# Attention phase of a Mamba and attention chain: second layer with keys on the partitions and a constant shift, head steps in pairs, own slots for the outer stages

## The chip, the core and the metric

The kernel runs on one core of one Trainium2 chip. Its engines are TensorE (PE in the profile, with PEld for its weight loads), VectorE (DVE), ScalarE (ACT), GpSimd (POOL) and SyncE (SP), which issues the DMAs. The metric is the device time of one execution in microseconds (us), the median of several.

## The reference, cut to what matters

Eight images of 256 channels and 32x32 pixels (1024 tokens) pass through four layers; all is float32.

```python
# layer 0: four Mamba blocks, a squeeze-and-excite gate, batch norm    (not touched)
# layer 1: four heads of 64 dimensions
attn = softmax(einsum('bihd,bjhd->bijh', q, k) * 64 ** -0.5, axis=2)
x = (einsum('bijh,bjhd->bihd', attn, v) @ w_out + b_out) + x
# layer 2: one head of 256 dimensions, on the negated energies
energy = einsum('bnc,bmc->bnm', x @ Wq.T + bq, x @ Wk.T + bk)
attention = softmax(max(energy, axis=-1) - energy, axis=-1)
x = gamma * einsum('bnm,bmc->bnc', attention, x @ Wv.T + bv) + x
# layer 3: position encoding, eight heads of 32 dimensions, output projection
x = x + pe;  out = softmax(q k / sqrt(32)) v;  y = out @ Wo.T + bo
```

A softmax doesn't change if one constant is subtracted from all the exponents of a row, so any shift that keeps the exponentials inside float32 gives the same result.

## The kernel before

`mamba_phase` computes layer 0 and spills each image to HBM. `attention_phase` then does layers 1 to 3 for all images in one interleaved stream. A recording layer (`Engines`, `InOrder`) keeps every engine's instructions in the order in which the program states them, and gives them all the line L48 in the profile; so the reader goes by tile names. SP alone is not held to that order.

**Stages.** `order` lists 16 calls of `heads`: layer 1 of image 0, layer 1 of image 1, layer 3 of image 0, layer 1 of image 2, layer 3 of image 1, and so on; the last two are layer 3 of images 6 and 7. Each call is called a stage here. Beside its heads a stage carries pieces of two generators: `ends(i)`, what follows the stage before it, and `begins(i)`, what the next stage needs. Beside the heads of layer 3 stand `residual` and the whole of `layer2` of the next image, and the loading, normalization and `qkv` projections of layer 1 of the image after it. Beside the heads of layer 1 stand `output` of the last layer 3 and `qkv` of the next.

**Heads.** 128 channels hold 2 heads of layer 1 or 4 of layer 3; `pairs` is 1 or 2. A step is one block of 128 keys (`kt`) for 512 queries (`half`) of one channel group (`m`), 32 steps in a stage. `weights` (part `"fs"`) multiplies keys by queries on 64 or 32 rows of the array for each head, the heads at the same time, into tiles `fs` of two PSUM banks (pool `ps_s`, 2 buffers), and ACT writes the exponentials `fp`. `product` (`"fo"`), one step later, multiplies values by `fp` on 64 or 32 columns of the array into the accumulator `fo` (pool `ps_o`, 4 buffers, shared with all projections), and sums `fp` over the key blocks into `fz`, on DVE for the first pair of heads and on POOL for the second. After 8 steps `divide` (`"z"`) sums `fz` over the partitions by a matmul with `ones` into `fzs`, takes the reciprocal `frec` on DVE, multiplies `fo` by it into the tile `fq`, and has POOL compare `frec` with two bounds into `ok`.

**Slots.** Between its parts, `heads` yields slot numbers, three for each step: `3 * i + 0, 1, 2`. In the middle stages `BESIDE_H` says at which slots the next piece of `end` or `begin` is put in; in the first two and last two stages the pieces of both are spread evenly, `PIECES = 52` for 96 slots. What is left over follows after the last slot. `PARTS_H` gives the order of the parts within a step, for 1 and 2 pairs.

**Layer 2.** `qkv` makes `fq` (the weights of query and key are multiplied beforehand into `wqk`, so x itself is the key) and `fv`. For each block of 128 queries, `energies` multiplies queries by keys into an `fs` tile with the queries on the partitions, and DVE takes the row minimum `fe`; `weights` has ACT compute the exponential with this minimum as its bias and the row sum; `scale` multiplies the row by gamma over the sum; `turn` transposes the row by eight transposes on TensorE (`ft`) and copies it (`fpt`); `product` multiplies by the values, 128 columns at a time, into `fo`, and DVE adds x. At the end POOL adds the position encoding, which makes x ready for layer 3.

At the end of the phase the minimum of `ok` becomes a flag; if a comparison failed anywhere, `general_attention` computes the three layers again in a form that takes a row maximum everywhere.

## Time and profile before

| | us |
|---|---|
| Median of 3 runs | 8681.78 (8677.01 to 8682.0) |
| Profiled execution | 8677.8 |
| Its span (first to last instruction) | 8676.0 |
| First attention matmul | 6272.8 |
| TensorE busy in the span | 8420.9 |
| DVE, POOL, ACT busy | 7188.4, 6924.9, 5504.7 |

The page's rows of 40 slices show each engine's busy share in tenths; a slice is 217 us here, and the attention phase begins at the 29th. A matmul in float32 stands as two instructions in the profile, and heads that run at the same time on parts of the array start 6 or 7 ns apart. The end of a matmul is modelled; the start of the next one is not, so lengths on TensorE are best read from start to start. In a line such as `fs<-fq,fk 64*128 64x512 f32 x4`, 64*128 is the part of the array (rows * columns), 64x512 the moving operand, x4 the number of instructions in a row.

### The profile page before, as it was taken

How to read it: one execution, taken by the hardware profiler on the slowest of the kernel's cores; microseconds unless marked ns; L12 is line 12 of the kernel's file. 1: busy time of each engine (PE TensorE's matmuls, PEld its weight loads, DVE VectorE, ACT ScalarE, POOL GpSimd, SP SyncE). 2: the span in 40 equal slices, each digit the busy share in tenths (PEclk: the TensorE clock that was granted, in tenths of full speed). 3: DMA queues.
4: the chain of work that ended last, by engine and by line, in shares of the span. 5: the costliest groups of instructions: out<-in, count | busy, mean ns of one | idle time of the engine just before them, and what ended most of it. 6: DMA issues, size and time to landing. Idle time of an engine off the chain costs nothing. (4 is left out here: it accounts for less than half of the span.)

```text
span 8676.0 us, 230366 instructions
## 1 busy us (share of the span) xinstructions
PE 8420.9 (97%) x100338; PEld 4366.5 (50%) x100338; DVE 7188.4 (83%) x7175; ACT 5504.7 (63%) x7805; POOL 6924.9 (80%) x2513
## 2 busy tenths in 40 slices
PE   8999999999999999999999999999799999999998
PEld 4555555555555555555555555555444344434432
DVE  5999999999999999999999999999755655565555
ACT  6777777777777777777777777777433334433434
POOL 5999999999999999999999999999713434343436
PEclk9999999999999999999999999999899999999999
DMA  3444444444444444444444444444400000000000
GB/s 116 130 130 128 127 133 134 130 129 128 131 127 129 134 131 130 127 132 126 128 134 133 127 144 140 138 135 138 145 1 6 10 6 8 8 6 6 3 3 11
DMA packets 558037, 841.33 MB, mean 97 GB/s; under 512 B 311328, under 2 KB 312416, under 8 KB 556384
## 3 DMA queue, kind: packets, MB, share of 16 engines
q1 hardware_dynamic: 557024, 826.52, 31.4%
q8 instruction: 795, 13.03, 0.6%
q14 instruction: 218, 1.79, 0.1%
HBM read 771.31 MB, written 55.05 MB: 95 GB/s over the span
## 5 line engine op out<-in xcount | busy, mean ns | idle before, releaser
L48 POOL TENSOR_TENSOR h<-h,ct 128x2048 f32<-128x2048 f32 x1022 | 4634.4, 4553 | 168.9 <-DVE hc L48 80.3
L48 ACT ACTIVATE da<-dt,A 128x512 f32<-128x512 f32 x4096 | 2641.7, 713 | 267.7 <-DVE h L48 267.0
L48 PEld LDWEIGHTS bx<-dg,dtxT 64*64 64x64 f32 x65536 | 1889.7, 133 | 1268.4 <-issue 1126.9
L48 DVE TENSOR_TENSOR_SCAN h<-da,hc,bx 128x512 f32<-128x512 f32 x2048 | 2454.8, 1261 | 61.3 <-PE bx L48 31.2
L48 DVE TENSOR_TENSOR_SCAN h<-da,bx 128x512 f32<-128x512 f32 x2048 | 2354.8, 1203 | 95.5 <-PE bx L48 77.0
L48 PE MATMUL bx<-dg,dtxT 64*64 64x128 f32 x65536 | 2221.8, 272 | 64.4 <-DVE h L48 34.7
L48 PE MATMUL y<-h,twin 64*64 64x512 f32 x16384 | 1956.4, 590 | 8.1 <-DVE h L48 4.7
L48 ACT ACTIVATE fp<-fs 128x1024 f32<-128x1024 f32 x768 | 759.5, 1021 | 1168.4 <-PE fs L48 1136.2
L48 PE MATMUL pin<-xn,win 128*128 128x512 f32 x2048 | 1005.7, 614 | 59.4 <-ACT sz L48 48.2
L48 PEld LDWEIGHTS y<-h,twin 64*64 64x64 f32 x16384 | 614.5, 133 | 631.3 <-issue 616.8
L48 POOL TENSOR_TENSOR fz<-fz,fp 128x1024 f32<-128x1024 f32 x192 | 485.1, 2526 | 434.2 <-ACT fp L48 430.2
L48 PE MATMUL fs<-fq,fk 32*128 32x512 f32 (+1 forms) x3072 | 636.7, 655 | 29.5 <-ACT fp L48 27.8
L48 DVE TENSOR_TENSOR fz<-fz,fp 128x1024 f32<-128x1024 f32 x384 | 597.8, 1557 | 77.8 <-ACT fp L48 69.1
L48 DVE SCALAR_TENSOR_TENSOR xin<-pin,vec,xin 128x509 f32<-128x509 f32 (+2 forms) x768 | 572.4, 745 | 61.3 <-ACT xin L48 21.9
L48 PE MATMUL fo<-fp,fv 128*32 128x512 f32 (+1 forms) x3072 | 563.6, 621 | 3.2 <-ACT fp L48 1.6
L48 PEld LDWEIGHTS pin<-xn,win 128*128 128x128 f32 x2048 | 349.9, 190 | 424.7 <-issue 282.8
L48 PE MATMUL po<-sz,wo 128*128 128x512 f32 x1024 | 486.5, 608 | 0.8 <-DVE sz L48 0.8
L48 ACT ACTIVATE sz<-pin,ib 128x512 f32<-128x512 f32 x256 | 175.8, 687 | 418.9 <-PE pin L48 418.9
L48 ACT ACTIVATE xin<-pin,cb,vec 128x512 f32<-128x512 f32 x256 | 199.0, 777 | 288.5 <-PE pin L48 288.5
L48 PEld LDWEIGHTS fs<-fq,fk 32*128 32x128 f32 (+1 forms) x3072 | 178.3, 187 | 391.8 <-issue 236.9
L48 POOL TENSOR_TENSOR e<-e,one 128x1024 f32<-128x1024 f32 x128 | 304.1, 2376 | 87.5 <-ACT one L48 84.1
L48 ACT ACTIVATE e<-pd,vec 128x512 f32<-128x512 f32 x256 | 176.1, 688 | 292.9 <-PE pd L48 290.8
(395 smaller groups left out, 8279.3 us busy)
## 6 DMA issues: line engine op xcount, KB each, us to landing
ct<-cdr SPq DMA_DIRECT2D x1024, 512.0 KB
dg<-diagonals SPq DMA_DIRECT2D x512, 256.0 KB
spill<-xo SPq DMA_DIRECT2D x64, 512.0 KB
x<-spill SPq DMA_DIRECT2D x48, 512.0 KB
xo<-spill SPq DMA_DIRECT2D x48, 512.0 KB
x<-in_x SPq DMA_DIRECT2D x16, 512.0 KB
res<-in_x SPq DMA_DIRECT2D x16, 512.0 KB
diagonals<-bt SPq DMA_DIRECT2D x512, 4.0 KB
```

What stands on the lines that cost most here:

```text
L48: return self.tc.keep_in_program_order(getattr(self.engine, name)(*args, **kwargs))
```

## The change

- **Layer 2** puts keys on the partitions. `weights` makes energies of two key blocks for 512 queries, and ACT writes exponentials `fp` with the constant `shift` of -40; row minimum, row sums, `scale` and `turn` are gone. `product` accumulates the output over the key blocks in two `ps_o` tiles of 512 columns, while POOL sums the exponentials; `divide`, once for each half of the queries, sums over the partitions with `ones` (now 128 columns wide), divides on DVE, and POOL adds x. Gamma is multiplied into the value weights and bias at the start of the phase, on ACT.
- **Heads** go through two steps per iteration, with six slots. In layer 1 the two `weights` stand together, ahead of the products; in layer 3 they stay apart. `divide` follows in the same iteration as the product that completes the sum.
- **The range test** keeps the least and the most of the sums themselves (`least`, `most`), on DVE, in place of POOL's four operations; the bounds are tested at the end.
- **Slots**: new lists for the middle stages, and lists of their own for the first two and the last two stages. The pool `fp` has 10 buffers in place of 8.

```diff
-PARTS_H = {1: ("fs", "z", "fo", "0", "1", "2"), 2: ("0", "fs", "fo", "z", "1", "2")}
+PARTS_H = {
+    1: ("fs0", "fs1", "fo0", "z", "0", "1", "2", "3", "4", "5", "fo1"),
+    2: ("0", "fs0", "fo0", "z", "1", "2", "3", "fs1", "fo1", "4", "5"),
+}
+
 
 BESIDE_H = {
-    3: (("end", (3, 5, 6, 8, 10, 14, 15, 15, 16, 22, 27, 28, 28, 28, 28, 29, 30, 42, 42, 42, 44, 48, 48, 50, 52, 54, 59, 59, 60, 62, 65, 66, 68, 69, 69, 75, 76, 76, 80, 83)),
-        ("begin", (40, 44, 50, 52, 55, 55, 63, 70, 78, 83, 86, 88, 91))),
-    1: (("end", (16, 16, 38, 41)),
-        ("begin", (37, 39, 43, 44, 52, 56, 64, 74, 79, 83, 87, 89))),
+    3: (
+        ("end", (2, 4, 7, 9, 12, 14, 17, 20, 23, 24, 24, 30, 34, 34, 36, 41, 44, 44, 46, 49, 51, 55, 55, 58, 60, 63, 65, 65, 71, 73, 79)),
+        ("begin", (24, 31, 39, 43, 54, 55, 66, 67, 70, 77, 86, 90, 92)),
+    ),
+    1: (
+        ("end", (10, 10, 26, 42)),
+        ("begin", (36, 43, 46, 46, 54, 57, 68, 75, 85, 85, 87, 88)),
+    ),
+    "first": (
+        ("begin", (10, 16, 22, 28, 34, 40, 46, 53, 59, 65, 71, 77, 83)),
+    ),
+    "second": (
+        ("end", (2, 2, 14, 20, 26, 26, 28, 29, 33, 36, 36, 36, 38, 39, 39, 39, 39, 45, 50, 50, 50, 51, 52, 54, 56, 56, 56, 61, 62, 63, 63, 63, 63, 64, 64, 65, 67, 71, 72)),
+        ("begin", (72, 72, 76, 76, 78, 88, 89, 89, 91, 93, 95, 97)),
+    ),
+    "late": (
+        ("end", (1, 2, 4, 7, 10, 10, 12, 14, 16, 19, 19, 22, 26, 29, 30, 30, 35, 36, 39, 40, 42, 43, 45, 45, 48, 48, 48, 50, 56, 58, 58, 60, 61, 61, 61, 61, 66, 66, 67)),
+        ("begin", (72, 77, 79, 86, 89, 89, 89, 91, 93, 97, 98, 102)),
+    ),
+    "last": (
+        ("end", (20, 22, 22, 46)),
+    ),
 }
-
-PIECES = 52
...
-    pp = ctx.enter_context(tc.tile_pool(name="f_p", bufs=8))
+    pp = ctx.enter_context(tc.tile_pool(name="f_p", bufs=10))
-    l2 = ctx.enter_context(tc.tile_pool(name="f_l2", bufs=2))
...
-    ones = cst.tile([P, 64], F32, name="ones")
+    ones = cst.tile([P, P], F32, name="ones")
     nc.gpsimd.memset(ones, 1.0)
-    ok = cst.tile([P, T], F32, name="ok")
-    nc.gpsimd.memset(ok, 1.0)
+    least = cst.tile([P, T], F32, name="least")
+    nc.gpsimd.memset(least, 1.0)
+    most = cst.tile([P, T], F32, name="most")
+    nc.gpsimd.memset(most, 1.0)
+
+    shift = cst.tile([P, 1], F32, name="shift")
+    nc.gpsimd.memset(shift, -40.0)
...
+    def extremes(z):
+
+        nc.vector.tensor_tensor(least, z, least, ALU.min)
+        nc.vector.tensor_tensor(most, z, most, ALU.max)
...
-        probs, acc = {}, {}
+        probs, acc, summed = {}, {}, []
...
-        def divide(i):
-            m, half, kt = steps[i]
-            if kt < TT - 1:
-                return
-            del probs[i]
+            if kt == TT - 1:
+                del probs[i]
+                summed.append((m, half))
+
+        def divide(m, half):
             z = ps_o.tile([P, T], F32, name=f"fzs{u}_{m}_{half}", tag="o")
             for h in range(2 * pairs):
                 r = h * D
...
             nc.vector.reciprocal(rec, z)
 
             nc.vector.tensor_tensor(q[:, m, half * T:(half + 1) * T], acc.pop((m, half)), rec, ALU.mult)
-            for op, bound in ((ALU.is_le, 1e25), (ALU.is_ge, 1e-37)):
-                f = sp.tile([P, T], F32, name=f"fok{u}_{m}_{half}_{bound}", tag="f")
-                nc.gpsimd.tensor_scalar(f, rec, bound, None, op)
-                nc.gpsimd.tensor_tensor(ok, ok, f, ALU.mult)
+            extremes(z)
 
         lag = LAG[pairs]
-        for i in range(len(steps) + lag + 1):
+        for i in range(0, len(steps) + lag + 2, 2):
             for part in PARTS_H[pairs]:
-                if part == "fs":
-                    if i < len(steps):
-                        weights(i)
+                if part[:2] == "fs":
+                    if i + int(part[2]) < len(steps):
+                        weights(i + int(part[2]))
+                elif part[:2] == "fo":
+                    if lag <= i + int(part[2]) < len(steps) + lag:
+                        product(i + int(part[2]) - lag)
                 elif part == "z":
-                    if 0 <= i - lag - 1:
-                        divide(i - lag - 1)
-                elif part == "fo":
-                    if lag <= i < len(steps) + lag:
-                        product(i - lag)
+                    for g in summed:
+                        divide(*g)
+                    summed.clear()
                 else:
                     yield 3 * i + int(part)
 
...
     def layer2(b, x):
+
         s = {}
         yield from qkv(2, b, x, bias2, None, s)
         q, v = s["q"], s["v"]
-        ps, ws, es, pts = {}, {}, {}, {}
-
-        def energies(t):
-            sc = ws[t] = ps_s.tile([P, 2, T], F32, name=f"fs2{b}_{t}", tag="s")
-            for half in range(2):
+        steps = [(half, a) for half in range(2) for a in range(TT // 2)]
+        probs, acc = {}, {}
+
+        def weights(half, a):
+            sc = ps_s.tile([P, 2, T], F32, name=f"fs2{b}_{half}_{a}", tag="s")
+            for j in range(2):
+                t = 2 * a + j
                 for m in range(CT):
-                    nc.tensor.matmul(sc[:, half, :], lhsT=q[:, m, t * P:(t + 1) * P], rhs=x[:, m, half * T:(half + 1) * T],
+                    nc.tensor.matmul(sc[:, j, :], lhsT=x[:, m, t * P:(t + 1) * P], rhs=q[:, m, half * T:(half + 1) * T],
                                      start=(m == 0), stop=(m == CT - 1))
-            e = es[t] = l2.tile([P, 1], F32, name=f"fe2{b}_{t}", tag="e")
-            nc.vector.tensor_reduce(e, sc, AX.XY, ALU.min)
-
-        def weights(t):
-            p = ps[t] = l2.tile([P, HW], F32, name=f"fp2{b}_{t}", tag="p2")
-            z = es[t, "z"] = l2.tile([P, 1], F32, name=f"fz2{b}_{t}", tag="z")
-            nc.scalar.activation(p, ws.pop(t).rearrange("p h t -> p (h t)"), AF.Exp, bias=es.pop(t), scale=-1.0, accum_out=z)
-
-        def scale(t):
-
-            z = es.pop((t, "z"))
-            nc.vector.reciprocal(z, z)
-            rz = l2.tile([P, 1], F32, name=f"frz2{b}_{t}", tag="rz")
-            nc.scalar.activation(rz, z, AF.Identity, scale=gamma)
-            nc.scalar.activation(ps[t], ps[t], AF.Identity, scale=rz)
-
-        def turn(t):
-            p = ps.pop(t)
-            pt = pts[t] = l2.tile([P, TT, P], F32, name=f"fpt2{b}_{t}", tag="pt")
-            for g in range(2):
-                tr = ps_o.tile([P, TT // 2, P], F32, name=f"ft2{b}_{t}_{g}", tag="o")
-                for j in range(TT // 2):
-                    kt = g * TT // 2 + j
-                    nc.tensor.transpose(tr[:, j, :], p[:, kt * P:(kt + 1) * P], ident)
-                nc.vector.tensor_copy(pt[:, g * TT // 2:(g + 1) * TT // 2, :], tr)
-
-        def product(t):
-            pt = pts.pop(t)
-            po = ps_o.tile([P, CT, P], F32, name=f"fo2{b}_{t}", tag="o")
+            p = probs[half, a] = pp.tile([P, 2, T], F32, name=f"fp2{b}_{half}_{a}", tag="p")
+            nc.scalar.activation(p, sc, AF.Exp, bias=shift, scale=-1.0)
+            yield
+
+        def product(half, a):
+            if a == 0:
+                acc["o"] = [ps_o.tile([P, T], F32, name=f"fo2{b}_{half}_{m}", tag="o") for m in range(CT)]
+            p = probs[half, a]
             for m in range(CT):
-                for kt in range(TT):
-                    nc.tensor.matmul(po[:, m, :], lhsT=v[:, kt, m * P:(m + 1) * P], rhs=pt[:, kt, :],
-                                     start=(kt == 0), stop=(kt == TT - 1))
-            nc.vector.tensor_tensor(q[:, :, t * P:(t + 1) * P], po, x[:, :, t * P:(t + 1) * P], ALU.add)
-
-        for i in range(TT + 2):
-            if i < TT:
-                energies(i)
-                yield
-            if 0 <= i - 2:
-                product(i - 2)
-            if i < TT:
-                weights(i)
-            yield
-            if 0 <= i - 1 < TT:
-                turn(i - 1)
-            if i < TT:
-                scale(i)
-            yield
-
-        nc.gpsimd.tensor_tensor(x, s["q"], pe, ALU.add)
+                for j in range(2):
+                    nc.tensor.matmul(acc["o"][m], lhsT=v[:, 2 * a + j, m * P:(m + 1) * P], rhs=p[:, j, :],
+                                     start=(a == 0 and j == 0), stop=(a == TT // 2 - 1 and j == 1))
+                if m == 0:
+                    yield
+            if a == 1:
+                acc["z"] = zp.tile([P, 2, T], F32, name=f"fz2{b}_{half}", tag="z2", bufs=2)
+            if a:
+                nc.gpsimd.tensor_tensor(acc["z"], acc["z"] if a > 1 else probs[half, 0], p, ALU.add)
+                probs.pop((half, a - 1))
+            yield
+
+        def divide(half):
+            z = ps_o.tile([P, T], F32, name=f"fzs2{b}_{half}", tag="o")
+            for j in range(2):
+                nc.tensor.matmul(z, lhsT=ones, rhs=acc["z"][:, j, :], start=(j == 0), stop=(j == 1))
+            rec = sp.tile([P, T], F32, name=f"fr2{b}_{half}", tag="rec")
+            nc.vector.reciprocal(rec, z)
+            sl = slice(half * T, (half + 1) * T)
+            for m in range(CT):
+                nc.vector.tensor_tensor(q[:, m, sl], acc["o"][m], rec, ALU.mult)
+            extremes(z)
+            nc.gpsimd.tensor_tensor(q[:, :, sl], q[:, :, sl], x[:, :, sl], ALU.add)
+            acc.clear()
+            del probs[half, TT // 2 - 1]
+            yield
+
+        for i in range(len(steps) + 1):
+            if i < len(steps):
+                yield from weights(*steps[i])
+            if i:
+                yield from product(*steps[i - 1])
+                if steps[i - 1][1] == TT // 2 - 1:
+                    yield from divide(steps[i - 1][0])
+
+        nc.gpsimd.tensor_tensor(x, q, pe, ALU.add)
         yield
 
...
+    nc.scalar.activation(w["wv2"], w["wv2"], AF.Identity, scale=gamma)
+    nc.scalar.activation(bv[2], bv[2], AF.Identity, scale=gamma)
     w["wq2"] = cst.tile([P, CT, C], F32, name="wqk2")
     bias2 = cst.tile([P, CT], F32, name="bias2")
...
         D = 64 if n == 1 else 32
         ends, nexts = end(i), begins(i)
-        regular = 0 < i and i + 1 < len(order) and order[i - 1][0] == order[i + 1][0] == (3 if n == 1 else 1)
-        both = chain(ends, nexts)
-        count = 0
+        kind = {0: "first", 1: "second", len(order) - 2: "late", len(order) - 1: "last"}.get(i, n)
+        rest = {"end": ends, "begin": nexts}
         for slot in heads(n, b, state[n, b], D, D ** -0.5):
-            if regular:
-                for (what, when), g in zip(BESIDE_H[n], (ends, nexts)):
-                    for _ in range(when.count(slot)):
-                        next(g, None)
-            else:
-                while count * 96 < PIECES * slot:
-                    next(both, None)
-                    count += 1
-        for _ in both:
+            for what, when in BESIDE_H[kind]:
+                for _ in range(when.count(slot)):
+                    next(rest[what], None)
+        for _ in chain(ends, nexts):
             pass
     for _ in output(B - 1, state[3, B - 1]):
         pass
 
 
+    ends = cst.tile([P, 2], F32, name="ends")
+    nc.vector.tensor_reduce(ends[:, 0:1], least, AX.X, ALU.min)
+    nc.vector.tensor_reduce(ends[:, 1:2], most, AX.X, ALU.max)
+    nc.vector.tensor_scalar(ends[:, 0:1], ends[:, 0:1], 1e-25, None, ALU.is_ge)
+    nc.vector.tensor_scalar(ends[:, 1:2], ends[:, 1:2], 1e37, None, ALU.is_le)
     low = cst.tile([P, 1], F32, name="low")
-    nc.vector.tensor_reduce(low, ok, AX.X, ALU.min)
+    nc.vector.tensor_tensor(low, ends[:, 0:1], ends[:, 1:2], ALU.mult)
     ps = ps_o.tile([P, T], F32, name="fcount", tag="o")
     nc.tensor.matmul(ps[0:1, 0:1], lhsT=low, rhs=ones[:, 0:1], start=True, stop=True)
     nc.vector.tensor_scalar(top, ps[0:1, 0:1], P - 0.5, None, ALU.is_lt)
```

## The prediction

> **What bounds the kernel now.** I read the page first, then the attention phase in windows, one for each stage of heads, then TensorE's timeline inside one stage of each kind.
>
> ```profile
> span 8676.0 us, 230366 instructions
> PE 8420.9 (97%) x100338; PEld 4366.5 (50%) x100338; DVE 7188.4 (83%) x7175; ACT 5504.7 (63%) x7805; POOL 6924.9 (80%) x2513
> PE   8999999999999999999999999999799999999998
> PEclk9999999999999999999999999999899999999999
> ```
>
> The change touches only what comes after the first attention matmul, at 6272.8 us; the rest of the span, 2403 us, is what it can move. There TensorE is at 9 tenths in every slice but the last. A busy TensorE can still hide lost time, so the windows come next.
>
> ```profile
> core 0: us, PE busy (x) PEld busy (x) DVE busy (x) ACT busy (x) POOL busy (x), PEclk, DMA share, GB/s
> 6299.06:6582.65 283.59, 276.97 (x1122) 116.88 (x1121) 150.46 (x148) 90.00 (x100) 50.29 (x29) 0.98 0.00 1
> 7351.93:7451.93 100.00, 99.44 (x354) 31.37 (x353) 65.56 (x52) 32.64 (x32) 31.19 (x17) 1.00 0.06 21
> 7451.93:7641.75 189.82, 186.58 (x1058) 88.49 (x1056) 104.86 (x100) 87.50 (x100) 91.30 (x44) 0.99 0.00 1
> 8319.62:8527.55 207.93, 194.71 (x1058) 89.91 (x1056) 103.12 (x100) 82.70 (x96) 97.58 (x45) 0.98 0.00 1
> 8527.55:8659.23 131.68, 108.47 (x565) 28.12 (x561) 75.58 (x40) 62.51 (x64) 106.00 (x44) 0.88 0.02 9
> ```
>
> The rows are: the first two stages (both layer 1); one layer 1 stage; one layer 3 stage (with layer 2 of another image beside it); the last but one; the last. Six middle stages of each kind alternate; layer 1 always takes 100.0, layer 3 188.2 to 191.2 (mean 189.5). In the middle no other engine is near its limit; only in the last stage is POOL (106.0 of 131.7) beside TensorE.
>
> ```profile
> 7062.12 1.99 PE L48 MATMUL fs<-fq,fk 64*128 64x512 f32 x8
> ...
> 7101.95 1.13 PE L48 MATMUL fs<-fq,fk 64*128 64x512 f32 x4
> 7103.01 1.08 PE L48 MATMUL fo<-fp,fv 128*64 128x512 f32 x4
> 7104.02 3.70 PE L48 MATMUL fwk<-fx,wk 128*128 128x512 f32 x8
> 7107.65 1.13 PE L48 MATMUL fs<-fq,fk 64*128 64x512 f32 x4
> ```
>
> Take start to start, not the modelled durations. A full-array `fwk` run of 8 instructions (each matmul is two) takes 3.63: 8 x 0.43 + 0.19. Two concurrent heads of `fs`, two passes: 1.06 = 2 x 0.43 + 0.2. So a pass of 512 columns costs 0.43 and each change of tile shape about 0.185. Where two `fs` steps stand together (7062.12, at a stage's start) no change lies between them. From the same spacing, `fwv` (256 columns) costs 0.216 and a 128-column instruction 0.11.
>
> **Check of the price list.** A middle layer 1 stage has (instructions taken from the built order) 136 passes of concurrent heads, 48 full passes, 32 of 256 columns and 73 shape changes: 184 x 0.43 + 32 x 0.216 + 73 x 0.185 = 99.5; measured 100.0. Layer 3: 136 + 128 passes, 64 of 256, 320 of 128 columns, 90 changes: 113.5 + 13.8 + 35.2 + 16.7 = 179.2 (summed from the finer spacings 178.4); measured 189.5, so 11 us of each are waits. The first two stages: 271.3 against 283.6. Last but one: 179.4 against 207.9. Last, with its tail: 85.8 against 148.4.
>
> **The change, TensorE's work.** Layer 2, per image: 64 transposes and 256 product instructions of 128 columns go (320 x 0.11 = 35.2); 64 product passes of 512 columns and 8 of `ones` come (72 x 0.43 = 31.0): -4.2. The energies only swap roles (64 passes both ways). Shape changes, counted in the built order: layer 1 middle 73 -> 48, as `fs0 fs1` stand together and `fo1` often meets the next iteration's `fs`/`fo`; first 71 -> 56; second 96 -> 62; layer 3 middle 90 -> 93 (its two steps are not merged, and the pieces are smaller); last but one 96 -> 90; last 67 -> 67. With 0.185 each: layer 1 -4.6 x 6; layer 3 -4.2 + 0.5 = -3.7 x 6; first -2.8; second -10.5; last but one -5.3: **-68** in all; the finer spacings give **-65**.
>
> **Waits, layer 3 middle.**
>
> ```profile
> 7503.00 1.13 PE L48 MATMUL fs<-fq,fk 32*128 32x512 f32 x4
> 7505.62 1.13 PE L48 MATMUL fs<-fq,fk 32*128 32x512 f32 x4 [1.50 <-ACT fp L48]
> 7506.68 1.79 PE L48 MATMUL fo<-fp,fv 128*32 128x512 f32 x8
> 7508.40 2.06 PE L48 MATMUL fs<-fq,fk 32*128 32x512 f32 x8
> ```
>
> Layer 2's energies hold one of the two `s` buffers until DVE's minimum and then the exponential are done (in this stage ACT waited 25.2 us in total for `fe`), so the heads' `fs` waits for a buffer. With the constant shift the exponential follows the matmul directly: this stall goes. What is late next: iterations with no piece between two `fs` (slots 25-27, 82-84, 94-96) where two exponentials of 1.02 outlast `fo`'s 0.9-1.0, up to 1 us each; the `ones` product behind POOL's last sum at the stage's end, about 2.4 with the wait of `fo` before it, as now; two places where layer 2's two accumulators, the heads' `fo` and a `fzs` hold all four `o` buffers until DVE has done reciprocal (3.36) and products (0.69 each). I take 7 of the 11 us (bounds 3 and 12): 175.2 + 7 = 182.2, **-44** over six.
>
> **Waits, layer 1 middle.** `z` now follows `fo0` directly. Before it PE has `fo`, `fs fs`, `fo0` = 4.8 us after the last `fs`; exponential and two DVE sums need 1.1 + 2 x 1.56 = 4.2, so it just fits; at the stage's end, where no `fs` is left, about 1 us shows. DVE per stage: 28 sums x 1.56, 4 x (3.36 + 0.69), the new extremes 8 x 0.69, 16 evacuations x 0.72, layer 2's last division 6.1: 83 of 95 us. I take 1.5 (0.5 to 4): 95.9, **-25** over six. DVE's new work hides under TensorE here; if DVE fell behind, each us would show.
>
> **First two.** The begin pieces no longer start at slot 0, where `fwq` waited 3.5 for x, then ran at half rate (8.6 in all). New: in the second stage, layer 2's `final` and the next `qkv` stand in one slot, 72. From the last `fzs2`: reciprocal 3.36, two products 1.38, POOL adds x (128x1024, 2.5) and the encoding (5.47): 12.7 us until x is there, with 4.8 us of TensorE work between; the stall is 8, and the clock adds to it. 258.0 + 3.7 + 12 = 273.7: **-10**.
>
> **Last but one.** Same chain, slots 66 to 72, and one head sum (2.53) ahead of the encoding in POOL's queue: 15.3 against 4.3: stall 11, with clock 15. The stretch without pieces that cost most of the 28 now has pieces: 174.6 + 7 + 15 = 196.6: **-11**.
>
> Here a rule is weighed. Row: after only 1.50 idle, `fo` and `fs` took 1.79 and 2.06 instead of 1.07 and 1.13, 1.6 us lost; after 3.62 (8609.25) 3.8. The Trainium skill, "TensorE: Matmul & The Clock Gate", Part 1, lets the clock halve only after an idle window of about 3.4 us and recover after a busy one as long: it would charge nothing for 1.5 us and at most 1.7 after a long stall. By it the two stalls and the last stage's four would cost some 10 us less, the sum -127. I keep the row.
>
> **Last stage.**
>
> ```profile
> 8598.18 1.49 POOL L48 TENSOR_SCALAR fok_1e+25_85807<-frec 128x512 f32<-128x512 f32 x1 [5.54 <-DVE frec L48]
> 8599.75 1.33 POOL L48 TENSOR_TENSOR ok<-ok,fok_1e+25_85807 128x512 f32<-128x512 f32 x1
> 8601.05 2.46 POOL L48 TENSOR_SCALAR fok_1e-37_85810<-frec 128x512 f32<-128x512 f32 x1
> 8603.59 1.27 POOL L48 TENSOR_TENSOR ok<-ok,fok_1e-37_85810 128x512 f32<-128x512 f32 x1
> 8604.82 3.32 POOL L48 TENSOR_TENSOR fz<-fp,fp 128x1024 f32<-128x1024 f32 x1
> 8608.22 17.30 POOL L48 TENSOR_TENSOR fz<-fz,fp 128x1024 f32<-128x1024 f32 x6
> ```
>
> A group of eight steps takes 33: DVE's reciprocal, 6.6 of checks, then 20.7 of sums, for which `fzs` waits. The checks leave POOL for DVE, so the sums start when two steps' exponentials are done, about 4 after `fzs`: 4 + 20.7 + 1.3 = 26, four times 104 (92 if DVE's sums disturb POOL's less, 112 if more): **-28**. `p` with 10 buffers lets ACT run a step further ahead; POOL still sets the group. The tail gains a second reduction, 0.7, and small operations: **+1**.
>
> At nothing: two gamma scalings on ACT (below 1.2) while TensorE still does `fwv` and `wqk`; the new DVE extremes, 160 x 0.69, against the 64 minima and 128 copies removed; layer 2's sums on POOL (48 x 2.53, 16 adds x 2.5), against 256 check operations removed. Moving x's load later moves no DMA: SP issues it behind the weights as before. Bounds for changed buffer places at the phase's start: -3 to +3.
>
> Sum: -10 - 44 - 25 - 11 - 28 + 1 = **-117**. The profiled execution took 8677.8 (span 8676.0), 4 below the median of the three runs, 8681.8; from the median: **8565**.
>
> **Rivals.**
> A, waits vanish: layer 3 keeps 3 (-24), stalls half (-13), last 92 (-12): 8516. For: the written slots leave few empty iterations. Chance 0.2.
> B, the waits return elsewhere: layer 3 keeps its 11 (+24), POOL's group falls only to 30 (+16), second and late stall 8 more: only the TensorE price remains, 8615. For: POOL gets layer 2's sums just where heads' `fz` queue. Chance 0.22.
> C, slower: `z` right behind `fo` makes TensorE wait at each of the 64 divisions. In layer 3, exponentials and POOL's sum need 2.1 + 2.53 after `fs`, with only 2.85 of own work between: 1.8, and 1.6 of clock. It decides from 117/64 = 1.8 each; with 3.4 at the 60 not yet counted, +204: 8769. Against: in the middle stages pieces stand before three of four. Chance 0.04.
> D, the sums leave 1e-25..1e37 and the general phase runs: from the reference's own inputs I find layer 2's shifted sums between 10^-2.7 and 10^22.8; chance 0.01.
>
> **Numbers.** The forecast has 0.53. The range goes from A to B, 8515 to 8618. A run of this kernel tells 0.2% (17 us) from no change: faster 0.93 (forecast, A and most of B), same 0.02 (the edge of C), slower 0.05 (C and D).
>
> **What would show it.** Right: `ft` and `fe` gone; layer 1 stages at 96, layer 3 at 182, `fs` x8 at 1.92; a stall of about 8 before `fwq` of image 0's layer 3 and 11 for image 7; last groups at 26. Wrong: layer 1 at 99 or above (merged `fs` still pays a change), layer 3 at 187 or above with `fzs` waiting for POOL, last groups above 30.

## The result and the profile after

The changed kernel takes 8573.06 us (median of 4 runs, 8569.88 to 8574.08) against 8679.4 for the kernel before, run beside it: a ratio of 0.9878, interval 0.9861 to 0.9895. Its profiled span is 8572.2.

First the page of the changed kernel, the lines that answer to those shown of before: span, busy times, and TensorE's two rows of slices.

```profile
span 8572.2 us, 226127 instructions
PE 8320.3 (97%) x98354; PEld 4193.2 (49%) x98354; DVE 7173.1 (84%) x7067; ACT 5398.9 (63%) x7615; POOL 6714.5 (78%) x2323
PE   8999999999999999999999999999889999999998
PEclk8999999999999999999999999999999999999999
```

The share of TensorE is the same 97%; what fell is its amount, by 100.6 busy us. Then the windows by stage of the changed kernel, in the order first two, a middle layer 1, a middle layer 3, last but one, last (columns: window, its length, then busy us of PE, PEld, DVE, ACT and POOL, granted clock, DMA share, GB/s).

```profile
6298.73:6572.93 274.20, 261.91 (x873) 98.03 (x872) 150.22 (x132) 75.48 (x76) 25.07 (x9) 0.98 0.00 0
7308.80:7403.98 95.18, 94.57 (x353) 33.69 (x352) 69.53 (x61) 31.03 (x32) 7.75 (x2) 1.00 0.06 23
7403.98:7585.76 181.78, 179.94 (x811) 64.78 (x809) 94.62 (x77) 75.68 (x76) 88.56 (x35) 1.00 0.00 1
8234.88:8438.74 203.86, 186.24 (x810) 66.03 (x808) 103.53 (x81) 71.23 (x72) 96.36 (x37) 0.97 0.00 1
8438.74:8554.64 115.90, 97.83 (x562) 25.82 (x561) 96.76 (x46) 62.23 (x64) 85.02 (x28) 0.93 0.03 10
```

| stage | before | predicted | after |
|---|---|---|---|
| first two | 283.6 | 273.7 | 274.2 |
| layer 3 middle, each of six | 189.5 | 182.2 | 181.8 |
| layer 1 middle, each of six | 100.0 | 95.9 | 95.2 |
| last but one | 207.9 | 196.6 | 203.9 |
| last | 131.7 | 104 | 115.9 |
| tail | 16.8 | 17.8 | 17.6 |

The six middle pairs gave 75 of the 104 us, where 69 was foreseen; the first two stages gave 9, as foreseen; the last two gave 20 where 39 was foreseen.

**A middle layer 3 stage.** TensorE's waits in the changed kernel, in the stage of the third window:

```profile
PE fzs L48 <- POOL fz L48: 1.1, 1, 1.1
PE fs L48 <- ACT fp L48: 0.3, 2, 0.2
PE fo L48 <- ACT fp L48: 0.2, 1, 0.2
```

The wait of 1.50 at `fs` is gone. Taken from start to start, as a mean over the six stages, layer 2's products and transposes took 37.2 us before; its products and `fzs` take 32.6 now, 4.65 less. The `fs` and `fo` of the heads take 2.6 less and the waits that the view shows 1.1 less; the other projections take 0.6 more. Together that is the 7.7 us of a stage. Part of the heads' 2.6 is the clock: before, TensorE stood at half clock for 2.8 us of a stage on average, and now never.

**The last stage.** DVE of the changed kernel in its last group of eight steps, then POOL, then TensorE (start, length, engine, operation, idle before and what ended it):

```profile
8525.56 3.36 DVE L48 RECIPROCAL frec<-fzs 128x512 f32<-128x512 f32 x1 [2.06 <-PE fzs L48]
8528.95 0.69 DVE L48 TENSOR_TENSOR fq<-fo,frec 128x512 f32<-128x512 f32 x1
8529.56 0.68 DVE L48 TENSOR_TENSOR least<-fzs,least 128x512 f32<-128x512 f32 x1
8530.16 0.68 DVE L48 TENSOR_TENSOR most<-fzs,most 128x512 f32<-128x512 f32 x1
8530.76 2.19 DVE L48 TENSOR_TENSOR fz<-fp,fp 128x1024 f32<-128x1024 f32 x1
8533.05 19.67 DVE L48 TENSOR_TENSOR fz<-fz,fp 128x1024 f32<-128x1024 f32 x6
```
```profile
8529.49 2.37 POOL L48 TENSOR_TENSOR fz<-fp,fp 128x1024 f32<-128x1024 f32 x1 [7.07 <-ACT fp L48]
8531.94 19.70 POOL L48 TENSOR_TENSOR fz<-fz,fp 128x1024 f32<-128x1024 f32 x6
```
```profile
8552.77 1.94 PE L48 MATMUL fzs<-fz,ones 128*32 128x512 f32 x8 [6.54 <-DVE fz L48]
```

Six sums take DVE 19.67 and POOL 19.70 in the same stretch, 3.28 each from start to start, though without the other engine a DVE sum lasted 1.22 and a POOL sum 2.35. The engines go in lockstep. POOL ends at 8551.64, DVE at 8552.72, and `fzs` follows DVE.

**The last but one.** TensorE of the changed kernel, then POOL:

```profile
8390.79 2.93 PE L48 MATMUL fwq<-fx,wq 128*128 128x512 f32 x3 [10.35 <-POOL fx L48]
```
```profile
8379.67 2.35 POOL L48 TENSOR_TENSOR fq<-fq,fx 128x1024 f32<-128x1024 f32 x1 [11.95 <-ACT fp L48]
8381.98 3.32 POOL L48 TENSOR_TENSOR fz<-fz,fp 128x1024 f32<-128x1024 f32 x1
8385.26 5.47 POOL L48 TENSOR_TENSOR fx<-fq,pe 128x2048 f32<-128x2048 f32 x1
```

This is the foreseen chain with the foreseen stall: residual, one head sum, encoding, then `fwq`.

**The second stage.** Its stall stands elsewhere than foreseen: DVE, POOL and TensorE of the changed kernel, one view each.

```profile
6517.40 3.36 DVE L48 RECIPROCAL fr<-fzs 128x512 f32<-128x512 f32 x1 [19.87 <-PE fzs L48]
6523.19 7.83 DVE L48 TENSOR_TENSOR fz<-fz,fp 128x1024 f32<-128x1024 f32 x2
```
```profile
6524.58 5.36 POOL L48 TENSOR_TENSOR fx<-fq,pe 128x2048 f32<-128x2048 f32 x1
```
```profile
6531.07 1.98 PE L48 MATMUL fzs<-fz,ones 128*64 128x512 f32 x4 [9.78 <-DVE fz L48]
```

Two head sums wait behind layer 2's reciprocal and then take 7.83 instead of 2.4. Most of that is the second sum: it lasts 5.33 and ends 1.1 after POOL's encoding, so it stood until the encoding was done. TensorE waits for that sum, at `fzs`, before it comes to `fwq`.

### The profile page after: what moved, and what is told of

Read it like the earlier page. It is cut to its first block, busy times and chain, and to the rows that moved or that the text cites. A ratio compares the mean times of both kernels' runs of the same rounds, so it can differ in the third digit from the quotient of the medians.

```text
span 8572.2 us, 226127 instructions
## 1 busy us (share of the span) xinstructions
PE 8320.3 (97%) x98354; PEld 4193.2 (49%) x98354; DVE 7173.1 (84%) x7067; ACT 5398.9 (63%) x7615; POOL 6714.5 (78%) x2323
## 5 line engine op out<-in xcount | busy, mean ns | idle before, releaser
L48 POOL TENSOR_TENSOR fz<-fp,fp 128x1024 f32<-128x1024 f32 x48 | 120.9, 2518 | 985.6 <-ACT fp L48 976.3
L48 POOL TENSOR_TENSOR fz<-fz,fp 128x1024 f32<-128x1024 f32 x224 | 583.9, 2609 | 353.8 <-ACT fp L48 349.9
L48 PE MATMUL fo<-fp,fv 128*32 128x512 f32 (+2 forms) x3584 | 782.9, 607 | 3.0 <-ACT fp L48 2.9
L48 DVE SCALAR_TENSOR_TENSOR xin<-pin,vec,xin 128x509 f32<-128x509 f32 (+2 forms) x768 | 572.5, 746 | 61.5 <-ACT xin L48 22.1
L48 PE MATMUL fs<-fq,fk 32*128 32x512 f32 (+1 forms) x3072 | 581.2, 634 | 4.5 <-ACT fp L48 3.0
L48 PEld LDWEIGHTS fo<-fp,fv 128*32 128x32 f32 (+2 forms) x3584 | 190.2, 127 | 524.4 <-issue 479.6
```

The costliest lines, as they stand in the source:

```text
L48: return self.tc.keep_in_program_order(getattr(self.engine, name)(*args, **kwargs))
```

## The experiments

The first `fs` came at 6288.8 to 6299.3 us in the profiled executions, before any stage that the edits touch; what moves it is open. So the table counts from there, in stages (L1 and L3: the mean of the six middle stages of layers 1 and 3). The ratio is to the kernel before, with its interval.

| kernel | median us | ratio | first two | L1 | L3 | last two and tail | from first `fs` |
|---|---|---|---|---|---|---|---|
| before | 8679.4 | 1 | 283.6 | 100.0 | 189.5 | 356.4 | 2377.0 |
| changed | 8573.06 | 0.9878 (0.9861 to 0.9895) | 274.2 | 95.2 | 181.8 | 337.4 | 2273.5 |
| unpaired | 8625.47 | 0.9942 (0.9925 to 0.9959) | 294.4 | 100.0 | 181.8 | 342.8 | 2328.0 |
| even slots | 8600.6 | 0.991 (0.9894 to 0.9927) | 286.0 | 95.2 | 181.8 | 350.5 | 2298.3 |
| old layer 2 | 8708.01 | 1.0036 (1.0024 to 1.0049) | 273.7 | 95.2 | 201.7 | 349.4 | 2404.5 |
| test on POOL | 8691.02 | 1.0019 (1.0013 to 1.0026) | 281.2 | 98.2 to 101.2 | 190.5 to 193.3 | 361.2 | 2391.1 |
| last sums on DVE | 8552.69 | 0.9863 (0.9847 to 0.988) | 274.2 | 95.2 | 181.8 | 319.6 | 2255.8 |
| encoding first | 8561.77 | 0.987 (0.9853 to 0.9886) | 269.0 | 95.2 | 182.2 | 330.2 | 2263.2 |
| both | 8545.47 | 0.9851 (0.9835 to 0.9868) | 268.9 | 95.2 | 182.2 | 312.8 | 2245.8 |
| all sums on DVE | 8545.84 | 0.9852 (0.9836 to 0.9869) | 268.9 | 95.2 | 182.1 | 314.0 | 2246.3 |
| later z | 8658.14 | 0.998 (0.9973 to 0.9988) | 276.6 | 95.2 | 196.6 | 331.6 | 2358.6 |
| later z, test on POOL | 8715.1 | 1.0045 (1.0028 to 1.0062) | 281.1 | 96.1 | 200.4 | 353.8 | 2414.2 |

**Unpaired.** Layer 1's steps are taken one at a time again. The edit moves `z` as well; the run "later z" below shows that its place alone changes nothing in a middle layer 1 stage.

```diff
-    1: ("fs0", "fs1", "fo0", "z", "0", "1", "2", "3", "4", "5", "fo1"),
+    1: ("fs0", "fo0", "0", "1", "2", "fs1", "z", "fo1", "3", "4", "5"),
```

> The changed kernel with the heads of layer 1 taken one step at a time again (parts fs0, fo0, 0, 1, 2, fs1, z, fo1, 3, 4, 5). My account, TensorE's price of shape changes: a middle layer 1 stage goes from 48 to 73 changes, the first from 56 to 74, the second from 62 to 88; at 0.185 us that is 4.6 x 6 + 3.5 + 5.1 = 36 us, so a span of about 8608, with layer 1 stages at 99.5 to 100 instead of 95.2 and layer 3 stages unchanged at 181.8. Rival: the layer 1 stages became shorter because POOL no longer runs its checks there and DVE's sums are faster; then they stay at 95 to 96 and the span within 5 us of 8572.

A middle stage went back to 100.02, as before the change. TensorE in it, the unpaired kernel, then the changed one:

```profile
7344.64 1.13 PE L48 MATMUL fs<-fq,fk 64*128 64x512 f32 x4
7345.70 1.08 PE L48 MATMUL fo<-fp,fv 128*64 128x512 f32 x4
7346.71 1.13 PE L48 MATMUL fs<-fq,fk 64*128 64x512 f32 x4
```
```profile
7066.57 1.99 PE L48 MATMUL fs<-fq,fk 64*128 64x512 f32 x8
7068.49 1.08 PE L48 MATMUL fo<-fp,fv 128*64 128x512 f32 x4
```

`fs` to `fo` 1.06, `fo` to `fs` 1.01; paired, `fs` x8 takes 1.92 for two steps. 25 changes of shape are worth 4.83, 0.193 each: the price list holds. Outside the middle, 20 came on in the first two and 5.4 in the last two stages, more than the list gives (8.6 and nothing). In the first two, TensorE idles 21.2 instead of 12.2: `fo` now waits 2.51 and 4.28; that the slots, written for the paired order, are the reason is likely but not shown. In the last but one it idles the same 16.9, but stands at half clock for 20.5 us instead of 10.2; so most of that loss is of the clock and not of the order.

**Even slots.** The first two and last two stages take their pieces evenly again; nothing else changes.

```diff
+        both, count = chain(ends, nexts), 0
...
+            if kind in (1, 3):
+                for what, when in BESIDE_H[kind]:
...
+            else:
+                while count * 96 < 52 * slot:
+                    next(both, None)
+                    count += 1
```

> The changed kernel with the pieces of the first two and last two stages spread evenly (52 for 96 slots, first all of end, then all of begin) as before the change. My account: the wait for x at the start of the first stage comes back (8.6 us with the clock), the last but one loses some 5 to 10 in iterations without a piece; span 8585 to 8590. Rival: own slots are worth nothing, because the stalls that cost most there (9.95 us before fzs in the second stage, 10.4 before fwq in the last but one) come from the chain from layer 2's last division to the encoded x, which even spreading shortens as well or better; then the span is at or below 8572.

24.8 us, more than expected: 11.8 in the first two, where TensorE waits 3.49 at `fwq` and 1.42, 5.67 and 9.78 at three `fzs`, and 13.1 at the end, with waits of 6.21, 6.35 and 4.73 at `fzs` in the last but one. The 9.78 stands with both sets of slots: the lists took the other waits away, not the encoding's.

**Old layer 2** in the new frame: query blocks, row minimum and transposes, the old list of the middle layer 3 stages, `fp` with 8 buffers; pairs, place of `z` and range test as changed. Some of layer 2's last pieces are merged, so that the lists of the second and the last but one stage fit.

> The changed kernel with layer 2 as before the change (row minimum, scaling, transposes, products of 128 columns; gamma not in the weights), with the old list of pieces in the middle layer 3 stages and 8 buffers of fp; in the second and last but one stage its last pieces are merged to 39 so that the lists fit. My account: TensorE's price +5.0 in the second, +3.0 in each of six layer 3 stages, +4.0 in the last but one = 27, and the stalls of fs behind the minimum, some 4 us in each of eight images; layer 3 stages 187 to 189, span about 8630. Rival: only the TensorE work counts (stages at 185, span 8600), since the stall came from the old order of z and not from the minimum.

Much slower than expected: 201.7 in a layer 3 stage, where the kernel before, with the same layer 2, had 189.5. The longest waits of TensorE in one such stage (us in total, times, longest):

```profile
PE fwq L48 <- issue: 3.2, 1, 3.2
PE fo L48 <- DVE fq L48: 2.2, 1, 2.2
PE fs L48 <- ACT fp L48: 1.5, 1, 1.5
PE fzs L48 <- DVE fz L48: 1.3, 2, 0.6
...
```

TensorE idles 10.6 in this stage, where it idled 2.7 in the stage of the prediction's window, and it stands at half clock for 10.2 us instead of 3.4. The wait of 1.5 at `fs` is back with the row minimum; the other three rows are new, and the stage is slower than before the change. So part of what this run takes away is the fit between slots and work, which it doesn't separate. The new lists of the middle stages and the ten buffers of `fp` were not undone by themselves; their share is open.

**Test on POOL.** The four operations on the reciprocal return, for layer 2 too.

```diff
-        nc.vector.tensor_tensor(least, z, least, ALU.min)
-        nc.vector.tensor_tensor(most, z, most, ALU.max)
...
+        for op, bound in ((ALU.is_le, 1e25), (ALU.is_ge, 1e-37)):
...
+            nc.gpsimd.tensor_scalar(f, rec, bound, None, op)
+            nc.gpsimd.tensor_tensor(least, least, f, ALU.mult)
```

> The changed kernel with the range test on POOL again: four operations on the reciprocal per division, for layer 2 as well, in place of DVE's least and most. My account: middle stages unchanged (95.2 and 181.8 within 0.5); in the last stage a group of eight steps goes from 29.3 to 31 to 33, because POOL's sums start later but DVE's earlier and fewer of them meet; span 8580 to 8588. Rival, the account of my prediction: POOL alone sets the group, its 6.6 us of checks come on top, groups of 36, span near 8600.

The largest miss of an expectation: 118 us from the first `fs`, more than the whole gain of 103.5. POOL at the end of a layer 3 stage of this kernel, then TensorE:

```profile
7618.80 1.49 POOL L48 TENSOR_SCALAR fok<-frec 128x512 f32<-128x512 f32 x1 [4.67 <-DVE frec L48]
7620.37 1.27 POOL L48 TENSOR_TENSOR least<-least,fok 128x512 f32<-128x512 f32 x1
7621.60 1.49 POOL L48 TENSOR_SCALAR fok<-frec 128x512 f32<-128x512 f32 x1
7623.18 1.26 POOL L48 TENSOR_TENSOR least<-least,fok 128x512 f32<-128x512 f32 x1
7624.40 2.35 POOL L48 TENSOR_TENSOR fz<-fp,fp 128x1024 f32<-128x1024 f32 x1
7626.82 4.76 POOL L48 TENSOR_TENSOR fz<-fz,fp 128x1024 f32<-128x1024 f32 x2
```
```profile
7631.63 2.08 PE L48 MATMUL fzs<-fz,ones 128*128 128x512 f32 x2 [4.19 <-POOL fz L48]
```

The tests of one head group stand ahead of layer 2's own sums in POOL's queue, and layer 2's `fzs` waits 4.19 for the last of them.

**Last sums on DVE.** In the last image's layer 3 POOL does no sums.

```diff
-                    add = nc.gpsimd.tensor_tensor if j else nc.vector.tensor_tensor
+                    add = nc.gpsimd.tensor_tensor if j and b < B - 1 else nc.vector.tensor_tensor
```

> In the last image's layer 3 (the last two stages do it for image 7 only: the last stage) the sums of both pairs of heads go on DVE; POOL does none there. Theory (in the changed kernel DVE's and POOL's sums take turns, 3.2 each, and each pair of sums needs 3.30; DVE starts them only after reciprocal, product and range test, 5.2): alone, a DVE sum takes 1.22 to 1.56, so two of them need 2.5 to 3.1, start to start; with 14 of them 17 to 22 and 6.5 ahead of them the groups fall from 29.3 to 24 or 26, the last stage from 115.9 to about 96 to 105, the time from 8573 to about 8553 to 8562. Rival (the group is set by something else, the exponentials or the order of the parts): no change, 8570 to 8576. Rival 2 (14 sums serial on DVE are slower than two engines in turn): slower, up to 8585.

17.8 us less at the end, as the theory had it: the last stage takes 98.2. The sums of DVE in this kernel in one group of eight steps, then the window of that group (PE first, DVE third, POOL last of the busy columns):

```profile
8489.58 2.35 DVE L48 TENSOR_TENSOR fz<-fp,fp 128x1024 f32<-128x1024 f32 x2
8491.84 13.71 DVE L48 TENSOR_TENSOR fz<-fz,fp 128x1024 f32<-128x1024 f32 x12
```
```profile
8483.30:8507.20 23.90, 23.79 (x148) 6.34 (x148) 21.63 (x19) 15.54 (x16) 0.00 (x0) 1.00 0.00 1
```

Twice as many sums end sooner: 14 take 16.1 on DVE alone, where 7 took 21.9 beside POOL. The group is 23.9 and TensorE is busy for 23.8 of it at full clock, so what is left there is TensorE's own order. Part of it is `fs` that waits inside its run: in the group before, the runs take 1.97 and 1.25 in turn, against 1.07.

**Encoding first.** x gets the encoding after the last energies; at the end POOL only adds x to the output, by halves.

```diff
-            nc.gpsimd.tensor_tensor(q[:, :, sl], q[:, :, sl], x[:, :, sl], ALU.add)
...
+            if half:
+                for h in range(2):
+                    hs = slice(h * T, (h + 1) * T)
+                    nc.gpsimd.tensor_tensor(x[:, :, hs], q[:, :, hs], x[:, :, hs], ALU.add)
...
+            if i == len(steps):
+                nc.gpsimd.tensor_tensor(x, x, pe, ALU.add)
...
-        nc.gpsimd.tensor_tensor(x, q, pe, ALU.add)
```

> In layer 2 the position encoding is added to x beforehand, on POOL, after the last energies were read; at the end only POOL's sums of x and the output remain, once for each half of the queries (the second half: two of 128x1024 at the end of layer 2). The chain from the last fzs2 to the next stage's fwq loses POOL's 5.4 of 128x2048. Theory (the stalls of 10.4 at fwq in the last but one stage and of 9.95 at fzs in the second come from that POOL instruction, at fwq as the awaited one, at fzs as one that holds up a DVE sum for 5.33): last but one 203.9 to about 196, second stage by 3 to 5 less, sum about -10 to -15: 8558 to 8563. Rival (stalls come from the length of the DVE part alone, reciprocal and products and the head sums before it): less than 3, 8570 to 8573. In the middle stages nothing waits for x: no change there.

5.2 and 7.2 us less where they were expected, but 0.4 more in each middle layer 3 stage, where no change was expected: 10.3 in all. TensorE at the two places, the kernel with the encoding first:

```profile
6524.33 1.98 PE L48 MATMUL fzs<-fz,ones 128*64 128x512 f32 x4 [5.67 <-DVE fz L48]
```
```profile
8371.63 1.98 PE L48 MATMUL fwq<-fx,wq 128*128 128x512 f32 x4
...
8381.00 1.92 PE L48 MATMUL fzs<-fz,ones 128*32 128x512 f32 x4 [5.32 <-DVE fz L48]
```

The stall of 10.4 at `fwq` is gone, but a wait of 5.3 at the next `fzs` takes half of its place: DVE's head sums, late behind layer 2's division and in turns with POOL's. So the encoding was one cause and DVE's own part, the rival, another.

**Both**, and **all sums on DVE** (the encoding first, and POOL without head sums in every layer 3 stage: `add = nc.vector.tensor_tensor`).

> Both edits, sums of the last stage on DVE and the encoding added first. They act in different stages, so the gains should add: about 8540 to 8550. If the sum is missed by more than 5, the two share a cause (POOL's load in the last two stages).

> The encoding added first, and in all layer 3 stages the heads' sums on DVE, none on POOL. DVE then gets 28 further sums in each layer 3 stage, at 1.22 to 1.56 each +34 to +44: from 94.6 busy to about 130 of 182; POOL goes from 75.7 to under 30. Theory (POOL and DVE lose time by taking turns, so moving work to DVE costs little): middle layer 3 stages stay within 181 to 184, time as with both edits, 8540 to 8560. Rival (DVE's evacuations and divisions now queue behind two sums a step, and the buffers of fo come free later): layer 3 stages 186 or more, +30 in all, 8575 to 8590.

The two gains add, 27.7 of 28.0: 8545.47, the fastest version here. The kernel with all sums on DVE does the same in 8545.84. Its middle layer 3 stage, and below it that of the kernel with both edits:

```profile
7398.53:7580.60 182.07, 181.19 (x811) 64.65 (x809) 113.20 (x105) 75.58 (x76) 21.43 (x8) 1.00 0.00 1
```
```profile
7400.36:7582.52 182.16, 180.21 (x811) 64.71 (x809) 91.46 (x77) 75.78 (x76) 90.29 (x36) 1.00 0.00 1
```

With 28 more sums, DVE is busy only 21.7 us longer, while POOL is busy 68.9 less, for the same stage. 34 to 44 was expected; but the 28 sums that DVE had already became shorter too, from 1.56 on average to 1.22, once POOL no longer ran its own.

**Later z**, with the range test on DVE and on POOL.

```diff
-    1: ("fs0", "fs1", "fo0", "z", "0", "1", "2", "3", "4", "5", "fo1"),
-    2: ("0", "fs0", "fo0", "z", "1", "2", "3", "fs1", "fo1", "4", "5"),
+    1: ("fs0", "fs1", "fo0", "0", "1", "2", "3", "4", "5", "z", "fo1"),
+    2: ("0", "fs0", "fo0", "1", "2", "3", "fs1", "z", "fo1", "4", "5"),
```

> The division is moved back: in layer 1 it comes behind the six slots, just ahead of fo1 (about one step later, as before the change); in layer 3 ahead of fo1 too, which is half a step later than in the changed kernel, and half a step earlier than before the change (with both of layer 2's accumulators in PSUM a whole step later would need five buffers of four). The range test stays on DVE. Theory (with the range test on DVE the early place costs only 0.5 in a layer 1 stage and 1.2 in a layer 3 stage): within 0.1% of the changed kernel, 8565 to 8580. Rival (the early place itself costs, by making TensorE wait at the divisions): layer 1 at 94.6 and layer 3 at 179, 8545 to 8555.

> The same later place of the division, and the range test on POOL with its four operations on the reciprocal, as before the change (for layer 2's divisions too). With the early place this test on POOL cost 108. Theory (POOL's four operations matter only because the division now comes at once and waits for a sum that queues behind them): layer 1 returns to 95 to 96 from 99.8, layer 3 from 191 to 183 to 186, the last two stages keep their loss of about 20: 8610 to 8625. Rival (POOL is short of time in itself in layer 3 beside layer 2's sums): layer 3 stays at 189 or above, layer 1 at 99: 8670 to 8690.

Layer 1 behaved as the theory said: the place of `z` alone changes nothing (95.2), and with the later place the test on POOL costs 0.9 and not 4.6. Over the whole phase it costs 55.6 us with the later place, against 118 with the early one: about half of its cost hangs on the early `z`. Layer 3 refuted both expectations: later is 14.8 slower in a stage, 8.9 of it idle time of TensorE, the rest mostly the clock, which stands at half for 10.2 us of each stage. TensorE's longest waits in one stage of the later `z` on DVE, and the place of one:

```profile
PE fo L48 <- DVE fq L48: 8.5, 2, 4.2
...
```
```profile
7538.97 1.06 PE L48 MATMUL fzs<-fz,ones 128*32 128x512 f32 x8
7544.27 1.94 PE L48 MATMUL fo<-fp,fv 128*32 128x512 f32 x8 [4.23 <-DVE fq L48]
```

Layer 2 now holds two of the four `o` buffers, the finished `fo` and its `fzs` the others (read from the program's order of buffers); the next `fo` follows directly and has no buffer until DVE's reciprocal (3.36) and product (0.69) are done. In the changed kernel the pieces and an `fs` stand between. So in layer 3 it is the early `z` that makes room for the two accumulators of the new layer 2. The last two stages gained 5.8 from the later `z` on DVE, against the theory of no change.

## Why the prediction was right, and where its steps failed

- **TensorE's price, first.** Right: the unpaired kernel returns the 4.83 that 25 changes were priced at (4.6). The counts of shape changes come out of the traces too: 73, 90 and 96 before and 48, 93 and 90 after in layer 1, layer 3 and the last but one, and 167 and 118 in the first two together.
- **Layer 1, 95.9.** Measured 95.2: the allowance of 1.5 for waits was too large, the traces show 0.6 of idle time. (The printed terms, 99.5 - 4.6 + 1.5, give 96.4; the 95.9 rests on finer spacings that are not printed.) DVE was busy 69.5 and not 83. The later `z` without a gain there shows that the early place is covered.
- **Layer 3, 182.2.** Measured 181.8, and right in its parts: 4.65 for layer 2's own work on TensorE (4.2 was foreseen), and the waits smaller by about 4. But "11 us of each are waits" was too much: in the changed stage the waits view has 1.6, some 2.3 more stand inside `fs` runs, and the list itself is about 3 short. It was as short for before, so the difference came out.
- **First two, 273.7.** Right to 0.5, by luck as to the place: `fzs` waited, not `fwq`. The term that failed is "4.8 us of TensorE work between": it took the two head sums on DVE as free, but they stand behind layer 2's division and then behind POOL's encoding. Moving the encoding away took 5.2.
- **Last but one, 196.6.** The stall was 10.4 for 11, and its clock about 1.6 for 4. The term "7" for all other waits failed: the view has 6.5 of them, mostly at `fzs`, but some 6 more stand inside `fs` runs, and about 5 are spread over spacings a little longer than the list. The stage ended 7.3 later.
- **Last, 104.** A group took 29.2 for 26, and the stage 115.9, outside the bounds of 92 and 112. In the last group POOL's first sum starts 5.9 after the `fzs` before it (5.3 was foreseen), its seven sums take 22.1 for 20.7, and DVE ends 1.1 after POOL. So two steps failed. "POOL still sets the group": DVE, now with the range test ahead of its sums, became the later one. And the sums of both engines now fall together: DVE's 28 sums took 77.7 us in this stage, against 56.8 before, and POOL's 85.0 against 81.1. The prediction had named this as its worse bound, "if more", but had sized it too small. The run with all last sums on DVE shows the cause: 23.9 instead of 29.2.
- **"At nothing": the checks off POOL.** Right for the step from before to after, as those stages came out, but not free in itself: with the new layer 2 and the early `z`, putting them back costs 118. The prediction had no such coupling in it.
- **The rivals.** A and B are out by the middle stages, C by layer 1 at 95.2; in layer 3 the early `z` even helps. B's picture, POOL's sums being late, comes near only in the last stage, where DVE's are later still. (B's printed terms, 24, 16 and 8, come to 8613 and not 8615.)

**The weighed rule.** The prediction kept to its row of the profile, a loss after only 1.50 us of idle time. The two windows below follow that same wait in two stages of the kernel before: the stage of the prediction's lines, then one that took 188.2. The granted clock is the third figure from the end.

```profile
7506.89:7510.30 3.41, 3.41 (x16) 0.52 (x8) 1.25 (x2) 0.99 (x1) 2.28 (x1) 0.50 0.00 0
6927.58:6931.00 3.42, 3.42 (x24) 1.06 (x28) 2.52 (x2) 2.08 (x3) 1.23 (x2) 1.00 0.00 0
```

The wait stands in all six middle layer 3 stages. In four the clock halved after it; in the two of 188.2 it did not. The trace shows a difference: the changes of the clock are multiples of 3.41 us apart, and in the four stages the wait lies inside one such period, in the two across the border of two. That is not the whole rule, for a wait of 1.62 inside one period (at 8492.66) was not followed by half clock. So what the row shows need not follow from the wait, but the whole idle window of the other rule was not needed either; there the measurement decides. On how much: when TensorE went on after the changed kernel's stalls of 4.4 to 10.4, it had 3.3 to 6.2 us of half clock still ahead. That is 1.7 to 3.1 us lost each if it is busy throughout (an estimate from the granted clock): below the row's 3.8, and mostly above the 1.7 that the prediction worked out from the rule.

The total forecast for the span, 8676.0 - 117 = 8559, was 13 too low: the last two stages gave 19 less than foreseen and the middle pairs 7 more. The median came closer, 8573 for 8565, since the changed kernel's profiled execution was not 4 below its median, as that of before had been. The range was wide enough to hold even a last pair of stages without any gain; that the time fell inside it says little of those terms.

The parts don't add. Undone one at a time, unpaired, even slots, old layer 2, test on POOL and early `z` cost 54.5, 24.8, 131, 118 and 85 from the first `fs`, four times the 103.5 that all brought together. Each such run prices a part inside the frame that was made for it.

## What to carry to other kernels

Cost sums that DVE and POOL do at the same time at the time of both together, not at either's own: here, with both operands in SBUF, a pair took 3.28 on two engines and 2.3 on DVE alone. A division that ends an accumulation has to stand well ahead of the matmul that next needs its buffer, and what stands in the same queue behind its slow reciprocal (3.36 here) has to be counted. Undoing one part of a joint change measures its fit to the others, not its share of the gain.

## What the runs showed of the hardware

DVE and POOL take turns with these sums: 1.14 a sum from start to start on DVE alone, 2.35 on POOL alone, 3.28 for the pair when both run, nearly the 3.49 of one after the other. A DVE sum that came behind POOL's 128x2048 addition lasted 5.33 and ended 1.1 after it, so it waited for the whole instruction. The Trainium skill, "SBUF — State Buffer", "Who interferes with whom", has the rule: a DVE instruction with two inputs in SBUF contends with a GpSimd instruction that reads SBUF, and the port pair that they share is an exclusive lock. This case's traces agree. The prediction gave this only a bound and should have weighed it.

The granted clock took two values in the attention phase, 1.0 and 0.5. The same wait of 1.50 us on TensorE was followed by a half-clock stretch in four stages of the kernel before, and by none in two. The changes come multiples of 3.41 us apart, and where in such a period the wait falls goes with the difference between the six; a rule that holds for every wait is not shown.
